# Clearing of the border tiles split over two engines, and half of the turned weights' copies moved to ScalarE

## The chip, the cores and the metric

The kernel runs on one core of one Trainium2 chip. The metric is the device time of one execution in microseconds, the median of several runs. Before the change that is 1867.02 us, from three runs of 1861.42, 1869.45 and 1867.02.

The engines are called by these names: PE is TensorE (matrix products), PEld its weight loads, DVE is VectorE, ACT is ScalarE, POOL is GpSimd, SP is SyncE, which here only issues DMAs. Each engine works through its own queue of instructions in order.

## The reference

The input x has 16 images of 256 channels and 56 x 56 pixels. Two residual layers follow each other, each on a group norm of 32 groups:

```python
x = x + conv(_gn(x))        # layer 0
x = x + attention(_gn(x))   # layer 1
```

Layer 0 takes the sign of its input, and convolves it three times (dilation 1, 3 and 5, 3 x 3 taps, four groups of 64 channels) with binarised weights: the sign of the weight less its channel's mean, times the channel's mean of absolute values.

```python
xq = bin_act(xb)
for i, d in enumerate(DILATIONS):
    wq = _bin_weight(w[i])
    y = lax.conv_general_dilated(xq, wq, padding=[(d, d), (d, d)], rhs_dilation=(d, d), feature_group_count=GROUPS, ...)
    y = y + cb[i] - move1[i]
    out = out + jnp.where(y >= 0, y, alpha[i] * y) + move2[i]
out = layer norm over channels of out
```

Layer 1 projects to q, k and v of 64 channels each, takes the 3 x 3 neighbours of k and v (zero beyond the border), adds a small learned convolution to each, does a softmax over the nine neighbours, and projects back to 256 channels.

## The kernel before

An image is laid out as two halves of 28 rows on the two halves of the 128 partitions, four channel groups one after the other. Each half is again cut into units u = 0 and 1. Work on an image has these steps: statistics and sign of x (one tile per channel group), the convolutions (four groups times three dilations, 36 matmuls each), a layer norm over channels, a second group norm folded into the q, k, v weights, q, k, v, the products of q with nine shifts of k, softmax, the sum over nine shifts of v, and the projection.

Every step is an op with an engine, a function that emits its instructions, and the things it reads and writes. A class `Plan` collects all ops of all images and emits them by a table of places, `ORDER`: one entry for each op of a stage, in the order in which the ops were made, plus `PERIOD` times the image's number. `emit` takes again and again the op with the lowest place among those whose predecessors have been emitted and whose buffers are free. Since every engine works in order, this fixes each engine's queue. What "reads" and "writes" say serves this order alone; the waits on the chip are made by the tile framework from the tiles that the instructions touch. A stage name ends with `^` for the first image and with `$` for the last.

PSUM has four tiles of two banks, `banks`. They are used in turn by all matmul results: a new one can be begun once the last reader of an old one is done.

What matters here happens before and in the first image:

- Lines 530 to 537: four sign tiles `sgn` (padded on all sides by five zeros, 128 x 2508 bf16), and one tile each for q, k and v (`qt`, `kt`, `vt`, f32). All seven are cleared by GpSimd at the very start, so that their borders are zero. The insides are overwritten for each image; the borders never are.
- Lines 1114 to 1128, stage `first`: ten small VectorE instructions compute constants from the parameters, `mv2` (L1124) and `identb` (L1125) among them.
- Lines 1130 to 1163, `means`: a round trip over TensorE (L1137, L1146, L1150, L1160) takes the channels' mean out of `mv2`.
- Lines 1167 to 1226, stage `weights`: the 12 weight blocks (group, dilation) are loaded in six pairs, p0 to p5, both blocks of a pair side by side on the partitions. For a pair, VectorE takes two sums (`sums`: L1185 to L1187), ScalarE the sign (L1191, `wz`), and then for each block TensorE turns the nine taps (`turn`: L1207 and L1214, into a PSUM tile), and VectorE takes the scales from that tile and copies the turned taps to `wconv` (`keep`: L1222 to L1224).
- Stage `start` (lines 611 to 703): for the first image, channel group by channel group, the load of x (L617), the sum (VectorE, L637), the squares (ScalarE, L643), the group's statistics (L587 to L607, with ScalarE's L603 and L604 in between), and the sign (ScalarE, L667), whose halo rows are exchanged by two DMAs (L679, L680). For the other images the sums, too, are taken by ScalarE's L643; those of the second image come in the midst of the first image's convolutions.
- `conv` (lines 706 to 763): 36 matmuls (L716) into a PSUM tile, then for dilation 1 ScalarE L735, L750 and VectorE L755; for dilation 3 VectorE L745, ScalarE L750, VectorE L755; for dilation 5 ScalarE L742, L750, VectorE L755 and GpSimd L761. The L755 is the last reader of the PSUM tile.
- `second`, lines 1228 to 1259: the loads and preparation of the attention's weights (L1232 to L1257).
- The q, k and v results are written to their tiles by ScalarE (L924, `evict`).

In the stage of the weights, the queues of the engines hold this order: ScalarE has the sign of p0, of p1, the squares of the first x tile, the sign of p3, of p2, then L603, L604 and the first sign L667. TensorE turns p0 (second block first), p1, then a block of p3, and the rest later among the statistics and the convolutions: a block of p5 and both of p2 ahead of the convolution at 48.34 us, both blocks of p4 (the second first) and the other of p5 behind the two convolutions of 53.47 to 59.45 us.

Of the kernel before, what the change touches and what calls it, by code (L numbers as in the profile page):

```python
# [72 lines left out]
class Op:  # L73
    def __init__(self, place, emit, bufs):
# [6 lines left out]
PERIOD = 1231  # L81
ORDER = {
    "conv0": (
        -682, -410, -359, -2832, -303, -327, -265, -333, -280, -264, -245, -1566, -289, -213, -969, -970,
        -319, -128, -2067, -24, -3260, -58, -18, -16, -1028, -3936, 5, 17, 18, 101, 198, -321, 208, -3768,
        197, 207, 182, -601, -3937, 20, -15, -19, -199, 30, -146, 111, -2560, 21, -394, -20, -152, -3331,
    ),
    "conv0$": (
        -685, -409, -2692, -2836, -277, -2837, -419, -253, 194, -189, 109, -866, -1791, -207, -131, -440,
        -4781, -30, -3248, 99, -154, -250, -557, -386, -2111, -2366, 32, -462, -149, -2080, 175, -1794,  # L90
        -2185, -2439, 121, 140, -6017, -1732, -220, -9, -641, 100, -155, 112, -1493, 147, -1733, 191, 240,
        149, -865, -2379,
    ),
    "conv0^": (
        -2099, -6338, -223, -5746, -1337, -3215, -66, -5779, -1241, -202, -65, -5786, -1673, 42, -67, -667,
        -358, 124, 92, 358, -3217, 123, 231, 234, -3216, 565, 167, 400, 401, -1668, 228, 318, 504, -54, 229,
        -13, 515, -1726, -288, 227, 402, -115, -71, 40, -72, 517, -1182, 702, -116, -769, -2031, 119,
    ),
    "conv1": (
        160, -122, -123, 185, 199, -740, 209, -834, 265, -287, 150, -2506, -1087, 320, 171, 170, -823, 333,  # L100
        -2428, 361, -1220, 326, -175, 180, -1339, 356, 319, 255, 254, -2493, 355, -1340, 394, -1221, 714,
        746, 632, -113, -2040, 412, -162, -296, -1322, 470, -3611, 514, -1195, 925, -1683, -2369, 905, -1995,
    ),
    "conv1$": (
        56, -644, -645, -1492, 306, -11476, -498, -11477, 418, 239, 237, -3613, 188, 148, 146, 190, -1497,
        248, -878, 152, -867, 292, 151, -2181, -2390, -2392, 192, 98, 66, -864, 773, -432, 813, -1612, 662,
        456, 455, -1613, -818, 419, -28, -29, 44, 774, -431, 816, -434, 953, 968, 284, 678, -660,
    ),
    "conv1^": (
        666, 513, 523, -1198, 726, -697, -757, 826, 776, 581, 725, 830, 871, 682, 522, 601, -2033, 828, 824,  # L110
        695, 832, 829, 724, 578, 835, 715, 711, 612, 609, -2032, 865, 831, 878, 811, 949, 902, 901, 1044,
        1106, 38, 717, 718, 827, 869, 815, 890, -2027, 922, -1136, -964, 940, 959,
    ),
    "first^": (-3247,),
    "fold": (
        1404, -2035, -892, -2087, -3779, -4755, -952, -4221, -7223, -9967, -564, -942, -953, 1414, -949,
        -562, 1455, 407,
    ),
    "fold$": (
        1238, 1089, 753, 927, 1174, 593, 772, 1298, 934, 929, 595, 268, 1484, 297, 648, 1286, 559, -6518,  # L120
    ),
    "fold^": (
        1395, -941, -2847, -582, -784, 793, 792, -861, -863, -1498, -846, 1074, 1037, 696, 1424, -847, 1481,
        1444,
    ),
    "load0": (310,),
    "load0$": (539,),
    "load0^": (744,),
    "load1": (771,),
    "load1$": (614,),  # L130
    "load1^": (-117,),
    "mean0": (
        301, -2124, -1860, -2389, 172,
    ),
    "mean0$": (
        336, 87, 139, -232, -216,
    ),
    "mean0^": (
        785, 930, 214, -4431, 979,
    ),  # L140
    "mean1": (
        719, 911, 1038, -307, 787,
    ),
    "mean1$": (
        1195, -3235, -3236, -1711, 913,
    ),
    "mean1^": (
        1117, -960, 960, -337, -336,
    ),
    "norm0": (  # L150
        -732, -3656, -2175, -2045, -918, -715, -713, -2918, -1358, -2461, -2300, -2373, -2332,
    ),
    "norm0$": (
        -967, -5586, -5587, -2008, -2009, -2388, -1206, -2970, -3775, -3776, -5599, -1156, -4352,
    ),
    "prod0": (
        -1147, 777, -1035, 1488, 156, -3123, 155, -1057, -1219,
    ),
    "prod0$": (
        963, -2462, 449, -6519, 957, -392, -6024, 421, 1095,  # L160
    ),
    "prod0^": (
        -191, 8, -2267, -2417, -1351, -1352, 444, 443, 442,
    ),
    "prod1": (
        -3102, -1021, -550, -1863, 1762, 342, 1588, -2118, 615,
    ),
    "prod1$": (
        1043, 665, 309, 1102, 1281, 244, -3472, 1119, 1163,
    ),  # L170
    "prod1^": (
        1793, 1806, 1135, -4432, 1792, -1577, -69, 348, -1895,
    ),
    "proj0": (
        2327, 2254, 2286, 373, 2370, -2325, 2451, 1869, 1844,
    ),
    "proj0$": (
        4987, -693, 3217, 1049, 3039, -1400, 2317, -1399, -580,
    ),
    "proj0^": (  # L180
        2456, 2318, 2168, 956, 2213, 403, 2375, 410, 2115,
    ),
    "proj1": (
        2596, 566, 2594, 728, 2595, 31, 2582, 972, 1998,
    ),
    "proj1$": (
        45573, -572, 3218, -571, 45772, -1396, 44708, -1395, -465,
    ),
    "proj1^": (
        2523, 2564, 2522, -2377, 2607, 2566, 2508, -689, 1823,  # L190
    ),
    "qkv0": (
        1478, 1384, 1477, 1415, 1433, 1700, 1699, 387,
    ),
    "qkv0$": (
        1002, 836, 582, 610, -2708, 1260, 689, 1285,
    ),
    "qkv0^": (
        1490, 296, 1491, 1487, 1457, 1703, 685, 732,
    ),  # L200
    "qkv1": (
        1526, 1505, 1454, 1464, 1390, 1702, 1622, 712,
    ),
    "qkv1$": (
        1016, 619, 661, -3365, -1116, 1193, -1989, 1750,
    ),
    "qkv1^": (
        1514, 1090, 1467, 206, 1432, 1716, 551, 1624,
    ),
    "root0": (  # L210
        -323, -2507, -2508, 269, 181, -248, 245, -4518, -2509, 325,
    ),
    "root0$": (
        -1114, -4877, -4950, -2612, -1167, -77, -803, -5143, -195, 480,
    ),
    "root0^": (
        675, 216, 215, -4430, 892, 917, 881, -4445, 939, 1020,
    ),
    "root1": (
        230, -453, 161, -555, 768, 847, 743, 786, 916, 1244,  # L220
    ),
    "root1$": (
        554, -859, -860, -826, 842, 1105, 841, -3528, -3551, 1178,
    ),
    "root1^": (
        618, 129, 526, -1441, 1196, 1206, 1214, -1468, -1169, 1250,
    ),
    "scale0": (
        -2391, 308, 742, -657, 311, 552, -655, 352, -518, -1336, 995, 1083,
    ),  # L230
    "scale0$": (
        -3616, -530, 790, -3617, 1003, 241, -3628, -807, 585, -793, 528, 1088,
    ),
    "scale0^": (
        810, -2704, 1097, -2294, 932, 891, 945, 931, 741, 961, 1045, 820,
    ),
    "scale1": (
        886, -1324, 1341, -426, -1325, 1353, -427, -1862, 700, -848, -1134, 721,
    ),
    "scale1$": (  # L240
        -1608, -1879, 693, -2047, 933, 1050, -258, 94, 303, 639, -285, 299,
    ),
    "scale1^": (
        814, -2794, 1299, 658, 1033, 1223, -3076, -276, 1064, -3077, 1199, 1092,
    ),
    "second^": (
        -533, -33, -269, -5855, 451, 670, -3184, -3197, -1840, -2841,
    ),
    "sign": (
        -2935, -620, -1699, -748, -537, -497, -768, -351, -1710, -526, -1611, -387,  # L250
    ),
    "sign$": (
        -1806, -587, -690, -884, -1173, -1643, -1644, -406, -940, -917, -851, -827,
    ),
    "soft0": (
        9, -22, 1683, -1162, 1642, 1681, -558, 1274, 1482, -2383, -2384,
    ),
    "soft0$": (
        -161, -12, 709, -1106, -1117, 710, 1919, 1868, 1855, 1035, 1034,
    ),  # L260
    "soft0^": (
        1489, 802, 1647, -95, 1075, 1663, -111, -1410, -1369, 1319, 1463,
    ),
    "soft1": (
        441, 1789, 2048, 1788, 2054, 2034, 798, -383, 2119, 2137, 343,
    ),
    "soft1$": (
        -1857, -1858, 882, -1233, 2421, 2422, 1504, 1503, 1507, 1506, -1172,
    ),
    "soft1^": (  # L270
        677, -14, 2019, 809, 1715, 2038, 1866, -567, 1065, 1992, 1188,
    ),
    "start^": (
        -854, -3067, -598, -1842, -4706, -3059, -2934, -2823, -589, -736, -1682, -1681, -4293, -4179, -4129,
        -3138, -588, -388, -541, -5501, -586, -532, -5502, -4128, -3068, -3064, -449, -668, -3186, -3187,
        -3169, -3168, -3181, -1702, -226, -523, -539, -5503, -481, -1363, -3182, -3183, -3105, -3754, -447,
        -225, -756, -3172, -3590, -633, -3642, -3227, -200, 288, -344, -1586, -224, -1338, -3228, -3229,
        -3211, -3212, -201, -73, -3204, -3205, -5781, -76, -85, -3206, -62, -568,
    ),
    "stats": (  # L280
        -1755, -1273, -1265, -1692, -1019, -872, -1573, -996, -832, -1698, -871, -772,
    ),
    "stats$": (
        -1727, -1368, -1559, -1883, -1776, -1654, -1805, -1349, -1361, -1807, -1215, -1183,
    ),
    "term0": (
        1553, 1554, 1552, 1536, 1566, 1565, 1629, 1621, 1610, 1609,
    ),
    "term0$": (
        1054, 1130, 1129, 1128, 1073, 1072, 1071, 996, 1028, 1027,  # L290
    ),
    "term0^": (
        1555, 1548, 1546, 1568, 1576, 1577, 1627, 1408, 1407, 1409,
    ),
    "term1": (
        1721, 1729, 1733, 1732, 1767, 1768, 1778, 1619, 1781, 1620,
    ),
    "term1$": (
        1053, 1259, 1019, 1127, 1175, 1258, 1131, 1980, 1979, 1978,
    ),  # L300
    "term1^": (
        1728, 1717, 1358, 1679, 1357, 1918, 1389, 1349, 1580, 1317,
    ),
    "value0": (
        1731, 436, 1766, 437, 1761, 1776, 434, 1760, 1775, 286, 1585, 1779, 285, -552, 2037, -373, 222, 1937,
# [143 lines left out]
def preact_conv_attention(  # L449
# [14 lines left out]
    nc = tc.nc  # L464
# [71 lines left out]
    for t in (*sgn, *qts, *kts, *vts):  # L536
        nc.gpsimd.memset(t, 0.0)
# [14 lines left out]
    def act(f, r, w):  # L552
        op("ACT", f, r, w)
# [865 lines left out]
```

## Time and profile before

| | us |
|---|---|
| median of three runs | 1867.02 |
| profiled execution | 1872.31 |
| its span, first to last instruction | 1870.5 |
| VectorE's row of constants L1118 begins | 3.78 |
| GpSimd's last memset (`vt`) ends | 13.75 |
| first `keep` on VectorE (L1222) begins | 18.94 |
| first convolution (L716) begins | 34.10 |
| a `keep` copy (L1224), 128 x 576 | 0.75 |
| a weights' sign (L1191), 128 x 576 | 1.32 |

The profile is of one execution. A row of its timeline gives the start in microseconds from the span's start, the duration, the engine, the source line, the operation, the tiles it writes and reads, and in square brackets how long the engine had been idle and what released it. The chain of waits follows the work that ended last back through what released each step. A granted TensorE clock of 1.00 is full speed; its mean over the span is 0.979, and it is 0.50 to 0.58 between 45 and 60 us.

The first 60 us in stretches (busy time of each engine):

| stretch, us | PE | DVE | ACT | POOL | granted clock |
|---|---|---|---|---|---|
| 0 to 10 | 0.00 | 6.31 | 1.28 | 9.47 | 1.00 |
| 10 to 20 | 6.06 | 9.21 | 5.66 | 3.75 | 1.00 |
| 20 to 30 | 1.96 | 9.55 | 4.46 | 0.00 | 1.00 |
| 30 to 40 | 8.10 | 8.06 | 6.21 | 0.00 | 1.00 |
| 40 to 50 | 6.18 | 8.49 | 9.97 | 1.89 | 0.78 |
| 50 to 60 | 8.02 | 6.61 | 9.08 | 0.00 | 0.54 |

A VectorE instruction that has been taken up and waits for something inside the engine counts as busy here; the 6.31 us of the first stretch are of that kind.

### The profile page before, as it was taken

How to read it: one execution, taken by the hardware profiler on the slowest of the kernel's cores; microseconds unless marked ns; L12 is line 12 of the kernel's file. 1: busy time of each engine (PE TensorE's matmuls, PEld its weight loads, DVE VectorE, ACT ScalarE, POOL GpSimd, SP SyncE). 2: the span in 40 equal slices, each digit the busy share in tenths (PEclk: the TensorE clock that was granted, in tenths of full speed). 3: DMA queues.
4: the chain of work that ended last, by engine and by line, in shares of the span. 5: the costliest groups of instructions: out<-in, count | busy, mean ns of one | idle time of the engine just before them, and what ended most of it. 6: DMA issues, size and time to landing. Idle time of an engine off the chain costs nothing.

```text
span 1870.5 us, 62125 instructions
## 1 busy us (share of the span) xinstructions
PE 1653.7 (88%) x27322; PEld 953.1 (51%) x27322; DVE 1570.8 (84%) x2217; ACT 1314.6 (70%) x1861; POOL 1408.7 (75%) x782
## 2 busy tenths in 40 slices
PE   4879899898999989898998989899898989989784
PEld 3546455454545545454554545455454545745341
DVE  8777979979797997979799797979979797997966
ACT  5988778677777867677786777778677787755320
POOL 2147769688686968868696886869688686967865
PEclk9799999999999999999999999999999999999897
DMA  7852655547475554647555464755547467223023
GB/s 178 200 113 43 143 123 122 126 93 155 96 158 111 124 126 92 149 102 155 115 120 124 96 151 101 156 113 124 123 94 150 101 147 172 62 69 74 11 61 69
DMA packets 102094, 217.03 MB, mean 116 GB/s; under 512 B 10816, under 2 KB 84672, under 8 KB 101568
## 3 DMA queue, kind: packets, MB, share of 16 engines
q1 hardware_dynamic: 101824, 213.06, 51.8%
q8 instruction: 214, 3.51, 0.8%
q14 instruction: 56, 0.46, 0.1%
HBM read 156.23 MB, written 51.38 MB: 111 GB/s over the span
## 4 chain that ended last, share of the span: by engine, by line
PE 53%; POOL 18%; DVE 16%; issue 6%; ACT 4%; DMA 1%; SPq 0%; POOLq 0%; DVEq 0%; ACTq 0%
PE banks L716 19%; POOL m L1070 13%; PE banks L906 12%; PE banks L980 9%; DVE m L1055 4%; PE banks L1044 3%; PE banks L769 3%; POOL xt L850 3%; PE banks L1087 2%; ACT banks L750 2%; DVE rl L755 2%; DVE ct L755 2%; POOL p L959 1%; POOL ct L761 1%; DVE m L1075 1%
## 5 line engine op out<-in xcount | busy, mean ns | idle before, releaser
L716 PE MATMUL banks<-sgn,wconv 64*64 64x392 bf16 x13824 | 656.7, 335 | 60.3 <-DVE m L1055 25.8
L716 PEld LDWEIGHTS <-wconv 64*64 64x64 bf16 x13824 | 442.8, 106 | 279.1 <-issue 94.7
L1070 POOL TENSOR_TENSOR m<-m 128x784 f32<-128x784 f32 x255 | 475.3, 1864 | 95.9 <-DVE m L1055 82.2
L959 POOL TENSOR_TENSOR p<-qt,kt 128x784 f32<-128x784 f32 x267 | 468.1, 1789 | 93.2 <-ACT qt L924 88.0
L750 ACT ACTIVATE banks<-banks,cbi,csc 128x784 f32<-128x784 f32 x384 | 370.3, 973 | 95.8 <-DVE ct L745 95.8
L761 POOL TENSOR_TENSOR ct<-ct,rl 128x784 f32<-128x784 f32 x125 | 233.3, 1866 | 252.7 <-DVE ct L755 147.8
L1044 PE MATMUL banks<-at,wv 64*64 64x392 f32 x2560 | 276.1, 510 | 56.5 <-DVE lv L821 22.6
L1055 DVE SCALAR_TENSOR_TENSOR m<-banks,vb,vt 128x784 f32<-128x784 f32 x288 | 289.6, 1022 | 25.4 <-POOL m L1070 17.6
L755 DVE SCALAR_TENSOR_TENSOR ct<-banks,oalpha,ct 128x784 f32<-128x784 f32 x256 | 258.1, 1026 | 17.1 <-ACT banks L750 16.4
L906 PE MATMUL banks<-xt,wf 64*64 64x392 f32 x3072 | 269.0, 491 | 0.0
L850 POOL TENSOR_TENSOR xt<-xt,ct 128x784 f32<-128x784 f32 x124 | 229.2, 1871 | 1.4 <-DVE ct L837 1.3
L980 PE MATMUL banks<-p,wk 64*64 64x392 f32 x2304 | 213.7, 489 | 2.8 <-POOL p L959 2.6
L742 ACT ACTIVATE rl<-banks,asc 128x784 f32<-128x784 f32 x128 | 116.7, 912 | 107.0 <-PE banks L716 103.0
L906 PEld LDWEIGHTS banks<-xt,wf 64*64 64x64 f32 x3072 | 131.2, 133 | 101.2 <-issue 68.3
L643 ACT ACTIVATE xh<-xh 128x1568 f32<-128x1568 f32 x120 | 180.6, 1507 | 0.7
L735 ACT ACTIVATE ct<-banks,mv,asc 128x784 f32<-128x784 f32 x128 | 128.5, 1004 | 73.0 <-PE banks L716 72.8
L755 DVE SCALAR_TENSOR_TENSOR rl<-banks,oalpha,rl 128x784 f32<-128x784 f32 x128 | 131.8, 1030 | 53.6 <-ACT banks L750 48.8
L1044 PEld LDWEIGHTS banks<-at,wv 64*64 64x64 f32 x2560 | 86.8, 134 | 176.3 <-issue 69.2
L745 DVE SCALAR_TENSOR_TENSOR ct<-banks,asc,ct 128x784 f32<-128x784 f32 x128 | 131.0, 1024 | 24.9 <-PE banks L716 21.3
L980 PEld LDWEIGHTS banks<-p,wk 64*64 64x64 f32 x2304 | 93.1, 133 | 93.4 <-issue 76.2
L854 ACT ACTIVATE ct<-xt,pr 128x784 f32<-128x784 f32 x128 | 120.2, 940 | 25.4 <-POOL xt L850 23.0
L1087 PE MATMUL banks<-m,wp 64*64 64x392 f32 x1024 | 106.4, 518 | 32.1 <-DVE m L1075 29.6
(115 smaller groups left out, 1870.6 us busy)
## 6 DMA issues: line engine op xcount, KB each, us to landing
xh<-in_x SPq DMA_DIRECT2D x248, 392.0 KB, 5.7
xt<-in_x SPq DMA_DIRECT2D x128, 392.0 KB, 9.2
out<-xt SPq DMA_DIRECT2D x128, 392.0 KB, 5.9
sgn<-sgn SPq DMA_DIRECT2D x128, 41.2 KB, 7.6
p<-in_w SPq DMA_DIRECT2D x12, 144.0 KB, 3.2
xt<-in_wk_parts SPq DMA_DIRECT2D x1, 1344.0 KB, 8.1
xt<-in_wv_parts SPq DMA_DIRECT2D x1, 1280.0 KB, 9.4
wq<-in_wqkv SPq DMA_DIRECT2D x1, 384.0 KB, 9.7
```

What stands on the lines that cost most here:

```text
L643: lambda func=func, col=col: nc.scalar.activation(inside(g) if b == 0 else image(xh), image(xh), func, accum_out=sums[:, col : col + 1]),
L716: nc.tensor.matmul(out=ps[q * GC : (q + 1) * GC, h, 0:SN], lhsT=wconv[h * GC : (h + 1) * GC, g, d, tap, :], rhs=sgn[g][h * GC : (h + 1) * ...
L750: lambda: nc.scalar.activation(n(), n(), AF.Relu, bias=cbi[:, g, s], scale=csc[:, g, s]),
L755: lambda: nc.vector.scalar_tensor_tensor(to.tile, n(), oalpha[:, g, s], to.tile, ALU.mult, ALU.add),
L761: lambda e: e.tensor_tensor(ct.tile, ct.tile, to.tile, ALU.add),
L850: lambda e, g=g: e.tensor_tensor(xt[:, g], xt[:, g], ct[g].tile, ALU.add),
L906: nc.tensor.matmul(out=ps[h * D : (h + 1) * D, q, 0:SN], lhsT=wf[q * GC : (q + 1) * GC, g, j, :], rhs=xt[q * GC : (q + 1) * GC, g, h, :], ...
L959: e.tensor_tensor(p.tile.rearrange("p x (r w) -> p x r w", w=W), _view(qt[:, 0, u * SN :], [(NU * SN + LANES, 2), (W, SR), (1, W)]), shift ...
L980: nc.tensor.matmul(out=ps[q * D : (q + 1) * D, h, 0:n], lhsT=wk[r, j, :], rhs=rhs, start=s == 0, stop=s == 9,)
L1044: nc.tensor.matmul(out=ps[h * D : (h + 1) * D, q, 0:SN], lhsT=wv[q * D : (q + 1) * D, j, :], rhs=at[q * D : (q + 1) * D, h, 0:SN], start=True,
L1055: lambda j=j, m=m, ps=ps: nc.vector.scalar_tensor_tensor(m.tile.rearrange("p x (r w) -> p x r w", w=W), _view(ps[:, 0, :], [(512, 2), (W, ...
L1070: lambda e, m=m, acc=acc: e.tensor_tensor(acc.tile, acc.tile, m.tile, ALU.add),
```

## The change

Three sign tiles are now cleared by VectorE, ahead of all that it does otherwise; GpSimd clears the first one. The clearing of q, k and v becomes an op of the plan on GpSimd, with "identb" among what it reads, and the evictions of q, k and v read its "border". `keep` is split: the scales stay on VectorE, and the copy of the turned taps is an op of its own, on ScalarE for the second block of each pair and on VectorE for the first.

The table gets 13 more entries (12 copies, one clear), the period goes from 1231 to 1243, and all places are numbered anew. Sorted by place, all old ops keep their order, and each new entry of the copies stands right behind that of its `keep`; in `weights` there are now nine entries for each pair: load, sums, sign, and twice turn, keep, copy.

```diff
-PERIOD = 1231
+PERIOD = 1243
...
     "second^": (
-        -533, -33, -269, -5855, 451, 670, -3184, -3197, -1840, -2841,
+        -2018, -535, -33, -271, -5910, 457, 680, -3213, -3227, -1856, -2867,
     ),
...
     "weights^": (
-        -2510, -2689, -881, -1839, -3066, -3474, -3065, -2511, -4979, -817, -3150, -2372, -1841, -2371,
-        -2512, -3160, -590, 41, -218, 39, -5828, -2513, -2002, -591, -527, -3161, -1341, -3185, -540, -3043,
-        -70, 187, 107, 186, -97, -559, -5519, -448, 200, -3427, 35, 81,
+        -2534, -2715, -887, -1855, -3094, -3093, -3506, -3092, -3091, -2535, -5027, -823, -3178, -2395,
+        -2394, -1857, -2393, -2392, -2536, -3188, -592, 41, -220, -219, 39, -5883, -5882, -2537, -2020, -593,
+        -529, -3190, -3189, -1354, -3215, -3214, -542, -3069, -70, 191, 110, 111, 190, -98, -97, -561, -5569,
+        -450, 204, -3459, -3458, 35, 81, 82,
     ),
...
-    for t in (*sgn, *qts, *kts, *vts):
-        nc.gpsimd.memset(t, 0.0)
+    for g, t in enumerate(sgn):
+        (nc.vector if g else nc.gpsimd).memset(t, 0.0)
...
-        act(evict, [ps, bf], [("qkv", j, u, n)])
+        act(evict, [ps, bf, "border"], [("qkv", j, u, n)])
...
                 nc.vector.tensor_tensor(asc[:, g, s], csc[:, g, s], alpha[:, g, s], ALU.mult)
-                nc.vector.tensor_copy(wconv[:, g, d, :, :], tv()[:, 0:9, :])
-
-            dve(keep, [tp], [("wconv", g, d), ("scales", g, d)])
+
+            dve(keep, [tp], [("scales", g, d)])
+            copy = nc.scalar.copy if e else nc.vector.tensor_copy
+            (act if e else dve)(
+                lambda g=g, d=d, tv=tv, copy=copy: copy(wconv[:, g, d, :, :], tv()[:, 0:9, :]),
+                [tp],
+                [("wconv", g, d)],
+            )
 
     plan.at("second", 0)
+
+    def clear():
+        for t in (*qts, *kts, *vts):
+            nc.gpsimd.memset(t, 0.0)
+
+    pool(clear, ["identb"], ["border"])
```

## The prediction

> **What bounds the kernel now.** I read the page's engine shares first, then its chain of waits, then the chain and the timeline of the first 130 us, since every edit acts once, before the loop over images has settled.
>
> ```profile
> PE 1653.7 (88%) x27322; PEld 953.1 (51%) x27322; DVE 1570.8 (84%) x2217; ACT 1314.6 (70%) x1861; POOL 1408.7 (75%) x782
> ...
> PE 53%; POOL 18%; DVE 16%; issue 6%; ACT 4%; DMA 1%; SPq 0%; POOLq 0%; DVEq 0%; ACTq 0%
> ```
>
> TensorE holds half of the chain, and no other engine is free enough for a small saving to show by itself. None of the shares is touched: the change moves three memsets and six copies from one engine to another and three memsets within GpSimd's queue, some 13 us of engine time in 1870. So the question is by how much the loop begins earlier or later; as all queues are in a fixed order, I take such a shift to be carried to the end one for one.
>
> The start, from the timelines of GpSimd and VectorE (start us, duration us, engine, line):
>
> ```profile
> 0.73 8.56 POOL L537 MEMSET sgn<- 128x2508 bf16 x4 [0.29 <-POOLq L1406]
> ...
> 3.78 6.94 DVE L1118 TENSOR_SCALAR oalpha<-pr 128x12 f32<-128x12 f32 x1
> ...
> 9.23 1.46 POOL L537 MEMSET qt<- 128x1632 f32 x1
> ...
> 10.79 0.56 DVE L1124 TENSOR_TENSOR mv<-mv,ac 128x4 f32<-128x4 f32 x3
> ...
> 12.75 0.16 DVE L1146 COPY g<-banks 128x1 f32<-128x1 f32 x1 [0.48 <-PE banks L1137]
> 12.84 0.75 DVE L1185 TENSOR_REDUCE g<-p 128x1 f32<-128x576 f32 x1
> ```
>
> L1118 handles 12 elements, and takes 6.94 us: it ends at 10.72, 0.03 us behind GpSimd's fifth memset (9.23 + 1.46 = 10.69). VectorE stood behind GpSimd's memsets, then worked almost without a gap from 12.75 to 38.45. That stall is what the change can remove.
>
> ScalarE in the same stage:
>
> ```profile
> 25.10 0.20 ACT L603 ACTIVATE g<-g 128x1 f32<-128x1 f32 x1 [3.94 <-DVE g L602]
> ...
> 27.08 1.65 ACT L667 ACTIVATE sgn<-xh,g 128x1568 bf16<-128x1568 f32 x1 [1.57 <-DVE g L662]
> ```
>
> It waits 3.94 us for VectorE: this is its slack between its first weights' sign at 13.81 and 31.8, but for small gaps of 0.18 and 0.28. Later it has little:
>
> ```profile
> 54.22 1.50 ACT L643 ACTIVATE xh<-xh 128x1568 f32<-128x1568 f32 x1
> ...
> 56.73 0.91 ACT L742 ACTIVATE rl<-banks,asc 128x784 f32<-128x784 f32 x1 [0.92 <-issue]
> 57.54 0.97 ACT L750 ACTIVATE banks<-banks,cbi,csc 128x784 f32<-128x784 f32 x1
> ...
> 59.97 0.47 PE L1207 MATMUL banks<-identb,wz 64*64 64x64 bf16 x18
> ...
> 60.57 0.98 ACT L750 ACTIVATE banks<-banks,cbi,csc 128x784 f32<-128x784 f32 x1 [0.55 <-DVE ct L745]
> ...
> 69.03 1.00 ACT L735 ACTIVATE ct<-banks,mv,asc 128x784 f32<-128x784 f32 x1 [1.22 <-PE banks L716]
> ```
>
> Its two idle times, 0.92 and 0.55, and the 1.22 at 69.03 are all it has from 54 to 70. The TensorE line is a turn of the fifth weight pair, p4; TensorE reaches it only behind the convolutions of 53.47 to 59.45.
>
> **The memsets.** No row shows VectorE clearing. Its rows go at one element per 1.05 ns (1781 ns for the 1568 of L637, 743 for the 576 of L1185), so 2508 elements are 2.76 us and three, with the overlap of 0.08 that such rows have, 8.1. The fastest row, L1238, does 256 elements in 280 ns; less the 0.14 that L1185 has over its slope that is 0.55 ns each, so 1.5 us and 4.3 for three. I take 8.1: GpSimd's own memsets take 0.83 ns per element for bf16 and f32 alike ((2190 - 1462) / (2508 - 1632)), so a narrow type brings a memset nothing there. VectorE then begins its constants at 0.73 + 8.1 = 8.8, not 3.69.
>
> The Trainium skill ("VectorE: DVE Perf Modes", section on zero memsets as uint32) speaks against this edit: a memset costs a cycle per element whatever the type, unless it is issued on four-byte words; an estimate by it is 2508 / 0.96 GHz, 2.6 us each and 7.8 for three, or half of that as words. No row here shows whether it holds. By it the sum would be 0.3 us better, or 4 with words.
>
> GpSimd clears one sign tile, then q, k and v: 0.73 + 2.12 + 1.40 + 1.52 + 1.60 = 7.4. The new op is ordered behind "identb" in the plan's table only: it reads no such tile, so I expect no wait on the chip, and it doesn't do what "behind the constants" says. At 7.4 it is over before VectorE gets to L1118 at 8.9, so that stall is gone. If the clear did wait, some 4.5 us of it would cover L1126 and L1186, at worst 4.5 us more. "border" on the qkv evictions comes far behind it: nothing.
>
> The constants, unstalled, take 1.05 us to the end of L1124 (0.32 from L1115 to L1122, 0.17, 0.56), so 9.85; the means' round trip over TensorE took 12.75 - 11.35 = 1.4, so L1146 starts at 11.25: **1.5 us earlier** than 12.75. The weights' sums follow at once.
>
> **Copies on ScalarE.** No row has this copy. L813 copies 196 elements from PSUM in 0.32 us, L742 scales 784 in 0.91; between them 576 take 0.70. Ends: 0.62, the same with the overlap of adjacent instructions, and 1.31, ScalarE's strided row L1191. I use 0.7. VectorE loses 0.67 six times, three of them before the first convolution.
>
> What counts more is the place. Each copy stands right behind its scales op in the table, so it comes into ScalarE's queue ahead of the next weights' sign, and waits there for the turn on TensorE (1.2 us: L1207 from 15.19 to the end of its L1214 at 16.38). Walk, first pair's sign ending at 15.13 - 1.5 = 13.6: turn to 14.85, copy to 15.6, second sign to 16.85, two turns to 19.2, copy to 19.95, squares of the first x tile (L643 and its accumulator) to 21.6, fourth pair's sign to 22.9, turn to 24.1, copy to 24.85, third pair's sign to 26.1. So L603 runs at 26.1, not 25.10. The sum again: waits 1.25 + 2.35 + 1.2 and copies 2.1 make 6.9; less the slack of 3.94, small gaps of 0.46 and the 1.5 gained, 1.0 late. VectorE is now early there and takes L605 at once (before it stood 0.4 behind a copy), so the first sign L667 is **0.6 us late**, and with it the reductions and squares behind it, up to the first convolution at 34.1. The 2.0 us taken from VectorE have become waiting.
>
> **The middle.** Of the other three copies, two wait for nothing. The one of pair 2 frees its PSUM tile 0.8 us sooner, so the convolution of 53.47 starts at 52.6. The third (pair 4, second half, place -97) goes ahead of the squares at 54.22 (place 212, now 216), and its turn comes only behind two convolutions, at 58.4 to 59.1. ScalarE, free at 55.65, idles 3.5 us, copies to 59.8, and then has L643, L742, L750, L643, L750, three L643, L735, L750 ahead of it: 1.55, 0.85, 0.9, 1.5, 0.9, 4.5, 0.9, 0.95 = 12.05 (starts to next starts), ending at about 71.8; before, that last L750 ended at 67.8. Behind it VectorE's L755 frees the tile for the fifth convolution of the run from 62.53, which at 9.54 / 5 us each began at 70.1 and now begins at 72.9, and ScalarE's L735 of 69.03 comes at 71.65, since its idle 1.22 us are used up. Its later gaps follow from its own results and move along. So **2.6 us late** (71.65 - 69.03), bounds 0 (all hidden) and 4.0 (ScalarE's whole delay, 71.8 - 67.8).
>
> **Sum.** +0.6 + 2.6 = +3.2 us. On the profiled execution, 1872.31 with a span of 1870.5, that is 1875.5; the runs' median is 5.3 below that execution, so 1867.0 + 3.2 = **1870.2**, rounded to 1870. Copies at 1.31 would add 0.6 each, up to 3.6; with memsets at 4.3 the sum is +1.4 to -0.6 (below).
>
> **Rivals.** First, fast memsets. VectorE is done at 5.0. If L1118 then stands behind GpSimd to 7.4 as it did to 10.69, L1124 ends at 8.1 and the start is 1.8 better than in my walk: +1.4. Unstalled it is 3.8 better: 1866.4. For it: L1238; against: no memset row here gains. Second, VectorE's relief counts in full: 1.5 + 2.0 at the start, and 0.8 at 53.47, so -4.3, 1862.7. For it: VectorE held the chain from 12.84 to 33.5; against: the queue order above. Third, on the slower side: VectorE's memsets stand behind GpSimd's run as L1118 did. They then start at 7.4 instead of 0.73, 6.7 later, and all else follows: +9.9, 1877; at 4.3 for the three it is +6.1. It decides from the moment the two engines clear at once, at 0.73. For it: L1118's row. Against: L1115, at 3.69 during a memset, took 0.17, so not every VectorE instruction waits.
>
> The Trainium skill ("SBUF — State Buffer", section on who interferes with whom) says a VectorE instruction with at most one SBUF input, outside the two-port modes, does not contend with GpSimd; a memset has none. That would rule the third rival out; L1115 against L1118 fits it, and no row here shows a memset.
>
> **Chances.** My case 0.55, fast memsets 0.17, relief 0.15, the lock 0.13. One measurement can tell about 0.5% (9.3 us) from no change; the first three end inside that, though the runs' own spread of 8 us takes a little out on either side, and half of the third rival lies beyond it. Faster 0.07, same 0.81, slower 0.12. The range 1862 to 1878 takes in the relief below and the lock above.
>
> **What would show it.** A VectorE MEMSET row of 2.7 us each from 0.73; L1118 short; L1146 near 11.2; ScalarE copies at 14.9, 19.2 and 24.1 with waits on TensorE; L603 near 26; an idle ScalarE of 3 to 4 us ahead of 59; the convolution of 70.1 two to three us late. I am wrong if the first convolution starts before 32, if ScalarE has no wait near 56, or if the loop's period changes, since nothing in it is edited.

## The result and the profile after

The changed kernel took 1872.36 us (median of 13 runs, 1870.92 to 1875.75); the kernel before, on the same chip, 1868.14 us (13 runs, 1861.42 to 1871.86). The ratio is 1.003, with a 95% interval of 1.0018 to 1.0041: slower by 3.4 to 7.7 us. Forecast were +3.2 us, 1870, and a range of 1862 to 1878.

The profiled execution of the changed kernel took 1871.04 us, with a span of 1869.3, so 1.3 us less than the one profiled before (1872.31). Why the traces seem to say the opposite of the runs is the main thing to be learnt here. First the page's line of busy times:

```profile
PE 1649.4 (88%) x27322; PEld 952.4 (51%) x27322; DVE 1565.2 (84%) x2214; ACT 1316.8 (70%) x1867; POOL 1402.3 (75%) x779
```

The shares are as before; ScalarE has six instructions more. The start, from the timeline (lines have moved by one or more: L1118 is now L1119, L1146 is L1147, L1222 is L1223):

```profile
0.73 2.19 POOL L538 MEMSET sgn<- 128x2508 bf16 x1 [0.29 <-POOLq L1418]
1.07 1.10 DVE L538 MEMSET sgn<- 128x1254 uint32 x1 [1.07 <-PEq L1418]
2.38 1.10 DVE L538 MEMSET sgn<- 128x1254 uint32 x1 [0.21 <-issue]
2.86 1.46 POOL L1238 MEMSET qt<- 128x1632 f32 x1
3.69 1.10 DVE L538 MEMSET sgn<- 128x1254 uint32 x1 [0.21 <-issue]
4.26 1.55 POOL L1238 MEMSET kt<- 128x1740 f32 x1
...
4.74 1.10 DVE L1119 TENSOR_SCALAR oalpha<-pr 128x12 f32<-128x12 f32 x1
...
7.87 0.16 DVE L1147 COPY g<-banks 128x1 f32<-128x1 f32 x1 [0.49 <-PE banks L1138]
```

VectorE's memsets are issued on four-byte words, half as many as there are elements, and take 1.10 us each; all three are over at 4.79. GpSimd's clears of q, k and v begin at 2.86, right behind the first sign tile: the plan's "identb" made no wait on the chip. L1119 ends at 5.84, again 0.03 us behind a GpSimd memset (4.26 + 1.55 = 5.81), but after 1.10 us and not 6.94. L1147 comes 4.9 us earlier than in the trace of before.

ScalarE, from its timeline up to the first sign (L668):

```profile
14.25 0.64 ACT L1229 CAST wconv<-banks 128x576 bf16<-128x576 f32 x1 [3.99 <-DVE csc L1223]
...
18.71 0.64 ACT L1229 CAST wconv<-banks 128x576 bf16<-128x576 f32 x1 [2.61 <-DVE csc L1223]
...
23.57 0.64 ACT L1229 CAST wconv<-banks 128x576 bf16<-128x576 f32 x1 [1.48 <-DVE csc L1223]
...
26.93 1.65 ACT L668 ACTIVATE sgn<-xh,g 128x1568 bf16<-128x1568 f32 x1 [1.21 <-DVE g L663]
```

The 4.9 us are gone: the first sign is at 26.93, against 27.08 before. Each copy has ScalarE waiting ahead of it, 8.1 us for these three. The square brackets name L1223 on VectorE, which only takes the scales out of the same PSUM tile, and not TensorE's turn.

Among the convolutions, again ScalarE, and below it TensorE's longest wait of that stretch:

```profile
52.45 0.64 ACT L1229 CAST wconv<-banks 128x576 bf16<-128x576 f32 x1 [1.29 <-DVE csc L1223]
...
57.25 0.64 ACT L1229 CAST wconv<-banks 128x576 bf16<-128x576 f32 x1 [1.17 <-DVE csc L1223]
58.45 0.64 ACT L1229 CAST wconv<-banks 128x576 bf16<-128x576 f32 x1 [0.56 <-DVE csc L1223]
58.98 1.51 ACT L644 ACTIVATE xh<-xh 128x1568 f32<-128x1568 f32 x1
...
70.81 1.02 ACT L736 ACTIVATE ct<-banks,mv,asc 128x784 f32<-128x784 f32 x1
```

```profile
72.03 3.15 PE L717 MATMUL banks<-sgn,wconv 64*64 64x392 bf16 x36 [4.52 <-DVE ct L756]
```

The squares that started at 54.22 start at 58.98, ScalarE's L736 comes at 70.81 in place of 69.03, and TensorE stands still for 4.52 us for a PSUM tile, the fifth convolution of its run.

Yet the first layer norm's L813 (now L814) starts at 104.8 us in both traces, and both go on in step: 127.7 and 127.5, 165.8 and 165.7, 493.9 and 493.9. Two things besides the change differ between these two executions. TensorE ran at half clock for 27.3 us of the first 105 before, and for 13.7 after; a second trace of the changed kernel, below, has 27.3 too. And the execution of before was an unlucky one, as the runs below show. That these two made the executions meet is read from the traces, and no run sets the clock.

### The profile page after: what moved, and what is told of

Same layout as the page of the kernel before. It is cut to its first block, busy times and chain, and to the rows that moved or that the text cites. A ratio compares the mean times of both kernels' runs of the same rounds, so it can differ in the third digit from the quotient of the medians.

```text
span 1869.3 us, 62119 instructions
## 1 busy us (share of the span) xinstructions
PE 1649.4 (88%) x27322; PEld 952.4 (51%) x27322; DVE 1565.2 (84%) x2214; ACT 1316.8 (70%) x1867; POOL 1402.3 (75%) x779
## 4 chain that ended last, share of the span: by engine, by line
PE 55%; POOL 17%; DVE 15%; issue 6%; ACT 5%; DMA 1%; SPq 1%; POOLq 0%; DVEq 0%; ACTq 0%
PE banks L717 19%; PE banks L907 13%; POOL m L1071 12%; PE banks L981 10%; DVE m L1056 4%; PE banks L1045 3%; PE banks L770 3%; PE banks L1088 2%; POOL xt L851 2%; ACT banks L751 2%; DVE rl L756 2%; DVE ct L756 2%; DVE m L1076 1%; POOL ct L762 1%; DVE ct L828 1%
## 5 line engine op out<-in xcount | busy, mean ns | idle before, releaser
L907 PEld LDWEIGHTS banks<-xt,wf 64*64 64x64 f32 x3072 | 130.4, 133 | 101.9 <-issue 70.0
L736 ACT ACTIVATE ct<-banks,mv,asc 128x784 f32<-128x784 f32 x128 | 128.4, 1003 | 71.2 <-PE banks L717 71.0
```

What stands on the lines that cost most here:

```text
L907: nc.tensor.matmul(out=ps[h * D : (h + 1) * D, q, 0:SN], lhsT=wf[q * GC : (q + 1) * GC, g, j, :], rhs=xt[q * GC : (q + 1) * GC, g, h, :], ...
```

## The experiments

They were run on three further chips, each beside the kernel before, whose median was 1863.8 to 1863.9 us on each.

| kernel | median us | ratio to before, 95% interval | L1146 | first convolution | first L813 |
|---|---|---|---|---|---|
| before, first trace | | | 12.75 | 34.10 | 104.8 |
| before_again | 1865.92 | 0.9999, 0.9984 to 1.0013 | 7.10 | 28.47 | 99.5 |
| changed, first trace | 1872.36 | 1.0030, 1.0018 to 1.0041 | 7.87 | 33.95 | 104.8 |
| after_again | 1873.88 | 1.0044, 1.0028 to 1.0059 | 7.87 | 33.96 | 107.4 |
| clears_only | 1862.69 | 0.9998, 0.9990 to 1.0007 | 7.87 | 29.22 | 96.8 |
| copies_only | 1872.29 | 1.0049, 1.0036 to 1.0062 | 7.10 | 33.19 | 106.4 |
| front_copies | 1869.64 | 1.0031, 1.0019 to 1.0043 | 7.87 | 33.96 | 101.7 |
| middle_copies | 1868.72 | 1.0027, 1.0017 to 1.0037 | 7.86 | 29.22 | 101.7 |
| p4_copy_only | 1868.25 | 1.0011, 0.9999 to 1.0023 | 7.86 | 29.22 | 101.9 |
| p2_p5_copies | 1868.62 | 1.0015, 1.0002 to 1.0028 | 7.87 | 29.23 | 99.7 |
| copy_ahead_of_scales | 1869.15 | 1.0019, 1.0005 to 1.0032 | 7.87 | 30.86 | 103.0 |
| late_clears | 1862.74 | 0.9987, 0.9974 to 1.0000 | 6.24 | 27.61 | 95.2 |
| late_clears_late_copies | 1864.12 | 0.9997, 0.9985 to 1.0009 | 6.19 | 29.10 | 96.4 |

The last three columns are starts, in us, in the one execution profiled of each, on the line that does in that kernel what the named line does before.

**The two halves of the change, each alone.** My theory after the traces was that the clears gain and the ScalarE copies give it back, by waiting at the head of ScalarE's queue. The rival was that the start is without effect by 104 us and the medians differ by TensorE's clock.

```diff
# clears_only: every copy on VectorE
-copy = nc.scalar.copy if e else nc.vector.tensor_copy
-(act if e else dve)(
+copy = nc.vector.tensor_copy
+dve(
# copies_only: all seven clears on GpSimd at the start, the clear op empty
-for g, t in enumerate(sgn):
-    (nc.vector if g else nc.gpsimd).memset(t, 0.0)
+for t in (*sgn, *qts, *kts, *vts):
+    nc.gpsimd.memset(t, 0.0)
```

> All twelve copies of the turned weights stay on VectorE, behind their scales; the clears stay as changed (three sign tiles on VectorE, q, k and v behind the first sign tile on GpSimd). The queue theory (the clears gain 4.9 us at L1146, from 12.75 to 7.87, and the six ScalarE copies give it back by waiting at the head of ScalarE's queue): nothing gives it back, so the first convolution starts at 34.1 - 4.9 = 29.2 to 30 and the time is 4 to 5 us below the kernel before, 1863 to 1864. The clock theory (what the start does is gone by 104 us, and the medians differ by the number of half-clock stretches of TensorE): first convolution as early, but the time within 2 us of the kernel before. The clears cost something (rival): above the kernel before.

> All seven clears on GpSimd ahead of all else as before, the clear op left empty; the six copies on ScalarE as changed. Queue theory: everything of the changed start comes 4.9 us later, so the first sign L668 starts at 26.9 + 4.9 = 31.8, the first convolution near 38.8, and the time is some 7 to 9 us above the kernel before (1875 to 1877). Clock theory: within 2 us of it.

Measured: clears_only has its first convolution at 29.22, as expected, but is no faster than the kernel before (0.9998). copies_only is 8.4 us above before in medians, as forecast, but not for the reason given: with the very same seven memsets ahead, its L1119 took 1.31 us and its L1147 came at 7.10, earlier than with the change. The clock theory falls, since copies alone cost 0.36 to 0.62%: copies_only had as much half clock in its first 105 us as the unaltered kernel in its second trace, next, 27.3 us in both, and its first L813 came 6.9 us later. My own theory falls in its first half: the clears gained nothing over the kernel before that its runs could tell. What then was the kernel before really like?

**The kernel before, profiled once more**, unaltered.

> The kernel before, unaltered, profiled once more. If the 6.94 us of L1118 are a matter of chance (in copies_only, whose first memsets are the same seven on GpSimd, L1118 took 1.31 us and L1146 came at 7.10): L1118 may be short here too, L1146 near 7.1, the first convolution near 28.5, and then a median like that of clears_only, 0 to 1 us apart. If the stall belongs to this kernel: L1118 near 6.9 and the first convolution at 34.1 again.

Its start in the timeline:

```profile
0.73 8.65 POOL L537 MEMSET sgn<- 128x2508 bf16 x4 [0.29 <-POOLq L1406]
...
3.87 1.21 DVE L1118 TENSOR_SCALAR oalpha<-pr 128x12 f32<-128x12 f32 x1
...
7.10 0.16 DVE L1146 COPY g<-banks 128x1 f32<-128x1 f32 x1
```

L1118 took 1.21 us, and not 6.94; the first convolution came 5.6 us earlier than in the first trace, and the execution took 1866.59 us against 1872.31, 5.7 less. So the long stall, which the prediction took as the kernel's property, is a matter of the single execution: L1118 ended at 5.08 here, near the end of the second of the four sign memsets, and at 10.72 in the trace of before, behind the fifth memset, that of `qt`. That VectorE got in between two of them I read from the four memsets' 8.65 us together in place of 8.56. How often it is missed can't be said from two profiles; 34 runs of the kernel before on this chip lie between 1861.04 and 1872.18. Of all 95 runs of it on the three chips 16 took more than 1868.1 us, and of the 35 runs of clears_only, late_clears and late_clears_late_copies none did. The 16 may be the stalled ones, but no profile shows that.

**The changed kernel beside it**, unaltered, on the same chip.

> The changed kernel, unaltered, beside the same runs of the kernel before as the others. If the copies on ScalarE set its time and the clears matter little: between front_copies (+5.7) and copies_only (+8.4) above the kernel before, 6 to 9 us, with the first convolution at 33.9 to 34. If its start is worth nothing: 0 to 2 us.

Measured: 1873.88 against 1863.89, ratio 1.0044, which is 8.2 us; the first convolution at 33.96. That is more than on the first chip (1.0030); the two intervals overlap. Its start is the same to 0.02 us as in the first trace of the changed kernel, but its first L813 comes 2.6 us later, at 107.4; TensorE was at half clock for 27.3 us of the first 105, and not for 13.7. So a difference of two or three microseconds between two single traces is no evidence here. The gap between the two unstalled traces, after_again and before_again, is 107.4 - 99.5 = 7.9 us at the first layer norm, and the runs have 8.2; half clock is 27.3 us in both. So what the change loses seems to be lost by then, though these two executions themselves ended only 6.3 us apart (1872.93 and 1866.59).

**Copies of the front and of the middle.**

```diff
# front_copies                      (middle_copies: (2, 4, 5))
-copy = nc.scalar.copy if e else nc.vector.tensor_copy
-(act if e else dve)(
+copy = nc.scalar.copy if e and i in (0, 1, 3) else nc.vector.tensor_copy
+(act if e and i in (0, 1, 3) else dve)(
```

> Clears as changed, ScalarE copies for the pairs 0, 1 and 3 only (those ahead of the first convolution); the others on VectorE. Queue theory: the first convolution at 33.9 as in the changed kernel, no ScalarE wait between 50 and 60, the rest as before: 0 to 1 us from the kernel before, 1867 to 1869. Clock theory: the same as the changed kernel, 1872.

> Clears as changed, ScalarE copies for the pairs 2, 4 and 5 only (those among the convolutions). Queue theory: first convolution at 29.2 to 30, then 2 to 4 us lost where ScalarE waits for the copies ahead of its squares, so 1 to 3 us below the kernel before, 1865 to 1867. Clock theory: the same as the changed kernel, 1872.

Measured: each group costs by itself, front_copies 1.0031 and middle_copies 1.0027, where I had expected the first to be nearly free; that expectation still counted from the stalled trace. Against clears_only, front_copies has its first convolution 4.74 us later and its first L813 4.9; middle_copies begins alike, and its first L813 is 4.8 later. Their sum is 9.7; after_again is 10.6 behind clears_only there. For middle_copies the clock could have a part in this: half clock was 23.9 us of its first 105, against 17.1 in clears_only and front_copies. But the two traces have the same half-clock time up to 68 us, and its fifth convolution, at 67.73 against 63.21, is 4.5 us late already.

**Which wait in the middle.**

```diff
# p4_copy_only                      (p2_p5_copies: i in (2, 5))
+copy = nc.scalar.copy if e and i == 4 else nc.vector.tensor_copy
+(act if e and i == 4 else dve)(
```

> Clears as changed, one copy on ScalarE: that of the second block of pair 4 (place -97, ahead of the squares in ScalarE's queue). Queue theory: ScalarE is done at 49.4 with what stands ahead of it and waits until that block's L1223 on VectorE near 54.1, so the squares that clears_only starts at 49.32 start at 54.7, L736 of 60.22 comes at 64.7, TensorE waits some 4.5 us before the convolution of 63.21, and the time is as far above clears_only as that of middle_copies, 4 to 6 us. If the cost of the middle is in ScalarE's extra work (0.54 per copy): 0.5 us.

> Clears as changed, two copies on ScalarE: the second blocks of pairs 2 and 5. Queue theory: they wait for their L1223 on VectorE near 47.6 and 52.3, the squares of 49.32 start at 53, L736 of 60.22 near 63.1, TensorE waits 2 to 3 us before the convolution of 63.21; the time is 2.5 to 3.5 us above clears_only, less than with p4 alone. Extra work alone: 1 us.

ScalarE and TensorE of p4_copy_only:

```profile
54.58 0.64 ACT L1229 CAST wconv<-banks 128x576 bf16<-128x576 f32 x1 [5.18 <-DVE csc L1223]
55.12 1.51 ACT L644 ACTIVATE xh<-xh 128x1568 f32<-128x1568 f32 x1
```

```profile
68.16 2.53 PE L717 MATMUL banks<-sgn,wconv 64*64 64x392 bf16 x36 [4.52 <-DVE ct L756]
```

One copy of 0.64 us makes ScalarE wait 5.18, puts off its squares from 49.32 to 55.12, and TensorE pays 4.52 of it at 63.6 to 68.2. In p2_p5_copies the squares start at 52.91 and TensorE's wait is 3.07, both close to what was worked out beforehand. The two costs don't add: together (middle_copies) the wait is 4.52 again, since the waits for pairs 2 and 5 are part of the time that ScalarE would wait for pair 4. The traces follow the queue theory; the times resolve little: the ratios, 1.0011 and 1.0015, have overlapping intervals, and that of p4_copy_only (0.9999 to 1.0023) reaches into that of clears_only (0.9990 to 1.0007). The medians, 1868.25 and 1868.62, stand 5.6 and 5.9 us above the 1862.69 of clears_only, on chips where the kernel before had the same median to 0.1 us; by the ratios it is 2.4 and 3.2 us. That the copy of pair 4 alone costs more than the other two, as expected, the times don't show.

**The order of the two readers of one PSUM tile.** The scales on VectorE and the copy on ScalarE both only read the tile that the turn wrote. For the second block of each pair I exchanged their places in the table, for instance:

```diff
-... -3506, -3092, -3091, ...
+... -3506, -3091, -3092, ...
```

> The changed kernel with each ScalarE copy one place ahead of its scales op on VectorE, in place of one place behind it. In the changed kernel each of the six copies starts within 0.2 us of the end of that block's L1223 on VectorE, though it needs only the turn on TensorE; the first waits until 14.25 for a turn done at 11.5. If that wait is made by the order of the two readers of one PSUM tile: the first copy starts at 11.6, the first sign L668 at 24 to 25 in place of 26.9, the first convolution near 31.5, and the time is 2 to 4 us below the changed kernel. If the copies wait for VectorE for another reason, the start stays as it is: 14.25, 26.9, 33.95.

```profile
11.54 0.64 ACT L1229 CAST wconv<-banks 128x576 bf16<-128x576 f32 x1 [1.29 <-PE banks L1215]
...
23.84 1.65 ACT L668 ACTIVATE sgn<-xh,g 128x1568 bf16<-128x1568 f32 x1 [1.21 <-DVE g L663]
```

The copy now starts right behind the turn, and the bracket names TensorE. The first sign is 3.1 us earlier, the first convolution is at 30.86, and the time is 1869.15 against 1873.88 for after_again beside it, 4.7 less. So the emission order of two reads was turned into a wait of ScalarE for VectorE, and this is about half of what the change lost. The other half stays: ScalarE still waits for the turns, 1.29, 2.42 and 1.29 us at the front, and 2.63 for pair 4. The first convolution is still 1.6 us behind the 29.22 of clears_only, and TensorE still waits 4.52 us for the fifth, which starts at 68.36.

**Versions that might beat both.** In late_clears GpSimd reads the last constant before it clears, so that no memset lies beside the constants, and all copies are on VectorE. late_clears_late_copies puts the front's three copies on ScalarE again, behind the first squares and behind pair 2's sign.

```diff
# late_clears: all copies on VectorE as in clears_only, no clears ahead of the plan,
# the first image's squares read "border" in the plan, and
 def clear():
+    nc.gpsimd.tensor_tensor(qts[0][:, 0, 0:NG], nbet, nbet, ALU.add)
-    for t in (*qts, *kts, *vts):
+    for t in (*sgn, *qts, *kts, *vts):
         nc.gpsimd.memset(t, 0.0)
# late_clears_late_copies: i in (0, 1, 3) on ScalarE, at the places
-... -3092, -3091, ... -2393, -2392, ... -3215, -3214, ...
+... -3092, -599, ... -2393, -598, ... -3215, -591.5, ...
```

> All copies on VectorE; GpSimd first reads the last constant (nbet, L1127), so that all seven clears come behind the constants on the chip too, and VectorE clears nothing. No memset runs beside L1118, L1125 and L1126: constants from 3.69, L1146 at 6.1 to 6.2 in place of 7.87 in clears_only, first convolution at 27.5 to 28, time 1 to 2 us below clears_only and 0 to 6 below the kernel before, by how often that one stalls. If the start's length is not what counts: the same as clears_only, 0 from the kernel before.

> late_clears with the copies of the second blocks of pairs 0, 1 and 3 on ScalarE, but behind work that is not waiting: the first two behind the squares of the first x tile, the third behind the sign of pair 2, where ScalarE idled 3.9 us. If the place in the queue is what costs, and VectorE bounds the start: VectorE is 2.0 us shorter and the first convolution comes at 25.6 to 26.6 in place of 27.61, the time 1 to 2 us below late_clears. If a copy on ScalarE costs wherever it stands: not below late_clears.

The start of late_clears:

```profile
3.87 0.17 DVE L1117 TENSOR_SCALAR oalpha<-pr 128x12 f32<-128x12 f32 x1
...
5.11 0.20 POOL L1235 TENSOR_TENSOR qt<-nbet 128x4 f32<-128x4 f32 x1 [4.67 <-DVE nbet L1125]
5.24 8.56 POOL L1237 MEMSET sgn<- 128x2508 bf16 x4
```

L1117 is 0.17 us long with no memset beside it, and the first L813 comes at 95.2, the earliest of all. The ratio is 0.9987, interval 0.9974 to 1.0000: the best of the versions tried, at the edge of what can be told from no change, and 0.6% below the changed kernel beside it. With the late copies nothing is gained: the first sign comes at 22.08, where late_clears has it at 20.59. That version lies at 0.9997.

Here the start of late_clears is bounded, by its profile, by something that no clear can move: its first squares (L642) wait 3.47 us for the landing of x and begin at 13.62. They wait for x in before_again (13.53) and clears_only (14.07), too. With the late copies they begin at 13.77, and there the profile names GpSimd's last sign memset, which ends at 13.75; so in this version the late clears may hold them up as well. Copies put behind them come at 15.31 and 16.57, and the next signs (17.11 in place of 15.16), and so pair 3's turn (18.49 in place of 16.71), are put off by 1.8 to 2.0 us: the two copies and 0.64 us of wait ahead of the second.

## Why the prediction was right, and where its steps failed

The direction and the main mechanism hold: the copies on ScalarE wait at the head of its queue, and that costs more than the engine time they take. The size holds less well: forecast were +3.2, and measured are +4.2 between the medians, +5.6 by the ratio, and +8.2 in after_again. Several steps were wrong, and that the sum came near at all was luck: it was counted from a stalled trace, and its errors went against each other. Between the two unstalled traces L736 comes 8.2 us later (71.76 in after_again, 63.53 in before_again), 5.5 of them at the front, where 0.6 were forecast, and 2.7 in the middle, where 2.6 were.

- **The memsets.** I took 2.76 us each, 8.1 for three; they take 1.10 each with starts 1.31 apart and are over at 4.79, which is 4.06 behind the 0.73 from which I counted. The fast bound of the range (1.5 and 4.3) was nearest. The Trainium skill ("VectorE: DVE Perf Modes", section on zero memsets as uint32) had it: the rows show words, 1254 in place of 2508, and an estimate by its one cycle per word (0.96 GHz) is 1.31 us, which is the distance of their starts. The prediction names the rule beside the sum and does not count with it.
- **The stall as the kernel's own.** The text took L1118's 6.94 us for granted and valued its removal at what the walk could use of it. In before_again it was 1.21. That the profiled execution stood 5.3 us above the median should have been asked about (the highest of the 13 runs is 1871.86, it took 1872.31); it was only carried as an offset.
- **The wait in front of the copies.** I had ScalarE wait for TensorE's turn alone (1.25, 2.35, 1.2). It waited for VectorE's scales as well: 3.99, 2.61, 1.48. At 4.9 us of gain with the waits that I foresaw, the first sign would have been far earlier than 27.08; it came at 26.93, where I had +0.6, so 27.7. Against the unstalled kernel before, whose first sign is at 21.4, the front is 5.5 us late. This is the step that was furthest off; two errors, memsets too slow and waits too short, nearly cancelled.
- **The middle.** The order was right in detail: the pair 4 copy ahead of the squares, the squares near 59 (59.8 forecast, 58.98 measured), TensorE's wait for the tile of the fifth convolution (from 70.1 to 72.9 forecast; it starts at 72.03, behind a wait of 4.52). But of the other two copies I wrote that they wait for nothing. They waited 1.29 and 1.17, and in p2_p5_copies these two alone put off the squares from 49.32 to 52.91. And the convolution behind pair 2's copy began 0.18 us sooner (48.40 in middle_copies, 48.58 in clears_only), where I had 0.8. The size 2.6 has two answers. Counted from the first convolution of its own trace, L736 starts 34.9 us behind it before (69.03 - 34.10) and 35.1 in before_again; it is 36.9 with the change (70.81 - 33.95), 37.8 in after_again (71.76 - 33.96) and 37.3 in middle_copies (66.52 - 29.22): 1.8 to 2.9 more, about the forecast. In clears_only it is 32.8 (62.00 - 29.22), and against that the middle's copies cost 4.5. TensorE's clock differs between these stretches: up to that L736 it was at half clock for 17.1 us in both traces of before, and for 10.2 in clears_only and in middle_copies. A slower TensorE may leave ScalarE more time for its waits, so that part of the copies' cost would be hidden in the first comparison; I read that from these rows, and no run tried it.
- **"Behind the constants".** Right: the clears of q, k and v ran from 2.86, and "border" made no wait.
- **The rivals.** Fast memsets were true, and worth nothing against the usual run. VectorE memsets held up by GpSimd's did not occur: they ran at 1.07 beside a GpSimd memset of 0.73 to 2.92. VectorE's relief of 2.0 us at the front can't be seen in any version; in late_clears_late_copies, too, it was eaten by waits.
- **One for one.** That a shift of the start is carried to the end fits the stall: 5.6 us at the first convolution, 5.7 in the two executions of the kernel before. Smaller shifts can't be followed so: late_clears has its first L813 1.6 us ahead of clears_only (95.2 and 96.8), and their medians are the same to 0.1 us.
- **The loop** keeps its pace, as said: between 127 and 494 us the two first traces differ by 0.2 us at most.

## What to carry to other kernels

An engine that has idle time can't take over an op for nothing where its queue is fixed: count how long the op at its place will wait for its input, and what of that engine's work stands behind it. Ask whether the tile has a second reader on another engine, and which of the two is emitted first, since that order can become a wait. And before a stall in one trace is made the prize of a change, compare that execution with the other runs, or profile it twice.

## What the runs showed of the hardware

- The same instruction stream showed a VectorE `TENSOR_SCALAR` of 12 elements behind GpSimd memsets at 6.94 us in one execution and 1.21 in another; without a memset beside it, 0.17. The Trainium skill ("SBUF — State Buffer", section on who interferes with whom) says that the loser of the shared port waits for a whole instruction; here it came behind four in a row, the longest 2.19 us, in one execution, and got in between two of them in the other. A VectorE memset took the same 1.10 us beside a GpSimd memset of 0.73 to 2.92 as beside the next one, and GpSimd's own took 2.19 as before: neither held up the other, as that section says of a VectorE instruction with at most one SBUF input.
- TensorE's half-clock stretches come in multiples of 3.4 us and differ between executions of one kernel: 13.7 and 27.3 us in the first 105 us of the changed kernel, whose first layer norms lie 2.6 us apart with the same start. The Trainium skill ("TensorE: Matmul & The Clock Gate", Part 1, on the HAM clock gate) tells of a free-running window of about 3.4 us and of half rate after an idle one, which agrees with these multiples; what sets the stretches off was not tried.
- The 576-element copy from PSUM takes ScalarE 0.64 us and VectorE 0.75.
